# One of four edge-weight multiplications of a step goes from VectorE to GpSimd, in three groups of four

## The chip, the cores and the metric

The kernel runs on one core of a Trainium2 chip. The metric is the device time of one execution, in microseconds. Five engines work side by side, each in the order of its own queue: TensorE (PE in the profile, with its weight loads as PEld), VectorE (DVE), ScalarE (ACT), GpSimd (POOL) and the DMA issuing queue of SyncE (SP).

## The reference

Four graph layers follow each other on `x` of 128 graphs x 64 nodes x 256 features, each as `x = x + layer(relu(layernorm(x)))`. Only the fourth matters here, an attention over 512 edges (`src`, `dst`) with four heads of 64 features:

```python
Xq = (H @ W_lin.T).reshape(bt, n, h, dh)
Xv = (H @ W_val.T).reshape(bt, n, h, dh)
e = jnp.einsum('behd,hd->beh', jax.nn.leaky_relu(Xq[:, src] + Xq[:, dst], 0.2), a)
e = e + jnp.log(A0[src, dst] + EPS)[None, :, None]
e_t = e.transpose(1, 0, 2)
m = jax.ops.segment_max(e_t, src, num_segments=n)
ex = jnp.exp(e_t - m[src])
attn = ex / jax.ops.segment_sum(ex, src, num_segments=n)[src]
Vt = Xv[:, dst].transpose(1, 0, 2, 3)
Y = jax.ops.segment_sum(attn[..., None] * Vt, src, num_segments=n)
return Y.transpose(1, 0, 2, 3).reshape(bt, n, d) @ W_out.T
```

## The kernel before

`layer3` computes the fourth layer in 32 steps of 4 graphs, in `NG` = 4 groups of 8 steps. The edges are sorted, and gathering or summing over them is done by matmuls with one-hot matrices: `S2` (both ends of an edge, `ed_S` in the profile), `OST` and `ODT` (source and destination, edges on the partitions, four chunks `c` of 128 edges).

In an iteration `g` of the loop the following is issued, for different steps at once:

- `score`: 16 matmuls `ps<-ed_S,Q` into 8 PSUM tiles, read by ScalarE into `r`; `reduce` sums `r` into `acc` (`acc<-r,ed_apad`).
- `normed`, `turned`, `queries` for later blocks of 8 graphs: layer norm, transposes (`ps<-ident,h`, copied to `hT`, then differences `hS` and `hT<-hT` on VectorE), and the seven products for `Q` and `XV`, added up on VectorE.
- At the end of a group `summed`, `softmax` and `edgewise`: scans over `sm_m` and `sm_e` on VectorE, then the weights `at` of the next eight steps, with edges on the partitions.
- Ten iterations later, for step `v = g - 10`: `spread` multiplies the edge weights `at` with the one-hot `OST` on VectorE, both broadcast, to four tiles `aw` of 128 x 1024 (chunk pair `c` in 0, 2, graph pair half `x` in 0, 1); `gathered` contracts them with `ODT` in 32 matmuls (`ps<-aw,ed_ODT`), which ScalarE copies to `an`; `weighted` (`ps<-an,XV`) and `output` (`ps<-w_o,y`) follow a step later, and VectorE adds the product to `X`, which a DMA on SyncE's queue writes out.

In `gathered` the tiles are read in this order: for `c`, for the chunk `k` of the pair, for `x`. The pool of `aw` has five buffers, so a step's four tiles take the fifth and the first three of those before them, and a tile is written when the gather that reads its buffer's former contents is over. All PSUM tiles `ps` share seven buffers in turn.

In most iterations the order of VectorE's instructions follows a scheduler's priorities, with a few held places (`hold`). TensorE, VectorE and ScalarE are wrapped in `Ordered`, by whose helper nearly all instructions carry the line L799; GpSimd is not wrapped. The last ten steps are written out in `turn`, where the issue order of the three wrapped engines is that of the program (`nc.ordered = True`); it begins with step 22 (`v = 8 * NG - 10`), so that the last two steps of the third group fall into it.

Of the kernel before, what the change touches and what calls it, by code (L numbers as in the profile page):

```python
# [11 lines left out]
ALU = mybir.AluOpType  # L12
# [1430 lines left out]
B, N, D = 128, 64, 256  # L1443
P = 128
# [5 lines left out]
NG = 4  # L1450
# [15 lines left out]
class Kernel:  # L1466
# [1253 lines left out]
    def spread(self, st, g, c, pool, vp, sp, rp, psum, psc):  # L2720

        at, i = st["at", g // 8], g % 8
        W = []
        for x in range(2):
            w = vp.tile([P, 2, 8, N], F32, name="aw", bufs=5)
            self.o.mul(w[:], at[:, c:c + 2, x, i].rearrange("p c m h -> p c (m h)")[:, :, :, None]
                       .to_broadcast([P, 2, 8, N]), self.OST[:, c:c + 2, None, :].to_broadcast([P, 2, 8, N]))
            W.append(w)
        return W

# [106 lines left out]
```

## Time and profile before

| | us |
|---|---|
| median of 3 runs | 2264.54 (2262.23 to 2266.95) |
| profiled execution, time | 2267.39 |
| profiled execution, span from first to last instruction | 2265.6 |
| TensorE busy | 2222.2 (98%) |
| VectorE busy | 1611.1 (71%) |
| ScalarE busy | 1143.9 (50%) |
| GpSimd busy | 7.3 (33 instructions, all but one in the first 43 us) |
| all 128 `aw` multiplications on VectorE | 150.3 (1.219 each) |
| mean granted TensorE clock | 0.996 |

Times in the profile's lines are microseconds from the span's start, unless marked ns. A line of a timeline gives start, time, engine, line of the kernel, operation, what is written and read (names of tiles, with the numbers of buffers left out), shape and count; in square brackets is the idle time of the engine before it and what ended that. A line of a waits or groups view gives the same for many instructions together. A line of the windows view gives, for a stretch, its length and the busy time of PE, PEld, DVE, ACT and POOL with the number of instructions, then the granted clock, the DMA engines' share and GB/s. Matmuls are pipelined, and a matmul that waits for a buffer can show as a longer block of matmuls instead of as idle time.

### The profile page before, as it was taken

The page shows a single profiled execution, that of the slowest core. Times are in us where ns is not written, and L with a number is a line of the kernel's source. Part 1 is how long each engine was busy: PE and PEld are TensorE (multiplying, and loading weights), DVE is VectorE, ACT ScalarE, POOL GpSimd, SP SyncE. Part 2 cuts the span into 40 slices and gives each one's busy share as a digit, 9 for nine tenths or more (in the row PEclk, how much of TensorE's full clock was granted, in tenths as well). Part 3 has the DMA queues.
Part 4 walks back from the last instruction along what each step waited for, and adds up shares of the span by engine and source line. Part 5 has one row for each costly group of instructions (what it writes and reads, how often), then busy time and mean ns, then how long its engine had stood idle before and what let it go on. Part 6 is the DMA issues. An engine that isn't in the chain of part 4 may idle for free.

```text
span 2265.6 us, 33653 instructions
## 1 busy us (share of the span) xinstructions
PE 2222.2 (98%) x12617; PEld 1619.5 (71%) x12617; DVE 1611.1 (71%) x4068; ACT 1143.9 (50%) x2499; POOL 7.3 (0%) x33
## 2 busy tenths in 40 slices
PE   7999998999999999999999999999999999999999
PEld 4554444667777778888999999888887555555554
DVE  8877576888438786676766766666965688778667
ACT  5667864764436663444444444334533664444431
POOL 1000000000000000000000000000000000000000
PEclk9999999999999999999999999999999999999999
DMA  6000210121000000000100002000002000000001
GB/s 180 1 1 13 73 56 23 66 94 38 1 28 1 1 19 1 1 1 1 38 1 1 1 1 75 1 1 5 13 1 75 1 1 15 15 20 20 15 25 48
DMA packets 61070, 54.88 MB, mean 24 GB/s; under 512 B 15203, under 2 KB 58724, under 8 KB 60900
## 3 DMA queue, kind: packets, MB, share of 16 engines
q1 hardware_dynamic: 60900, 52.66, 7.5%
q8 instruction: 101, 1.65, 0.3%
q14 instruction: 69, 0.57, 0.1%
HBM read 35.86 MB, written 16.78 MB: 23 GB/s over the span
## 4 chain that ended last, share of the span: by engine, by line
PE 78%; DVE 4%; ACT 1%; issue 1%; ACTq 0%; DVEq 0%
PE ps L799 71%; PE pt L799 4%; PE acc L799 3%; DVE sm_m L799 1%; PE pe L799 1%; DVE aw L799 1%; DVE X L799 1%; DVE XV L799 0%; ACT ls_g L799 0%; ACT h L799 0%; DVE ls_g L799 0%; DVE lin_p L799 0%; DVE lin_s L799 0%; DVE hT L799 0%; DVE sm_e L799 0%
## 5 line engine op out<-in xcount | busy, mean ns | idle before, releaser
L799 ACT ACTIVATE ls_g<-ls_g,ls_b 128x512 f32<-128x512 f32 (+4 forms) x472 | 243.2, 565 | 154.7 <-DVE ls_g L799 152.9
L799 ACT ACTIVATE ls_g<-ps,ls_b 128x256 f32<-128x256 f32 (+3 forms) x268 | 115.3, 470 | 335.6 <-PE ps L799 332.5
L799 PE MATMUL ps<-z,w 128*128 128x512 f32 x512 | 257.2, 624 | 0.0
L799 PE MATMUL ps<-big,X 128*128 128x176 f32 (+3 forms) x848 | 212.7, 366 | 0.1
L799 DVE TENSOR_TENSOR ls_g<-ls_z,ps 128x512 f32<-128x512 f32 (+5 forms) x256 | 146.9, 579 | 91.6 <-PE ps L799 90.0
L799 PE MATMUL ps<-ls_tx,X 128*128 128x160 f32 (+2 forms) x960 | 206.8, 326 | 1.5 <-DVE ls_tx L799 0.9
L799 PE MATMUL ps<-X,X 128*128 128x160 f32 (+1 forms) x896 | 199.0, 306 | 0.0
L799 PE MATMUL ps<-X,ls_w 128*128 128x256 f32 x640 | 190.4, 379 | 0.0
L799 PEld LDWEIGHTS ps<-ls_tx,X 128*128 128x128 f32 x960 | 161.7, 190 | 16.4 <-DVE X L799 4.8
L799 DVE TENSOR_TENSOR aw<-at,ed_OST 128x1024 f32<-128x1024 f32 x128 | 150.3, 1219 | 28.7 <-PE ps L799 28.5
L799 PEld LDWEIGHTS ps<-big,X 128*128 128x128 f32 x848 | 146.0, 190 | 29.7 <-issue 19.4
L799 ACT ACTIVATE r<-ps 128x512 f32<-128x512 f32 x256 | 129.3, 625 | 63.0 <-PE ps L799 63.0
L799 DVE TENSOR_TENSOR X<-ls_g 128x1024 f32<-128x1024 f32 (+2 forms) x108 | 117.4, 1087 | 49.8 <-ACT ls_g L799 49.8
L799 PEld LDWEIGHTS ps<-X,X 128*128 128x128 f32 x896 | 148.5, 190 | 0.0
L799 PE MATMUL ps<-X,ls_s 128*128 128x256 f32 x480 | 142.3, 379 | 0.0
L799 PEld LDWEIGHTS ps<-z,w 128*128 128x128 f32 x512 | 87.6, 191 | 67.8 <-issue 60.6
L799 PE MATMUL ps<-ls_tx,ls_s 128*128 128x256 f32 x464 | 134.7, 379 | 0.0
L799 PEld LDWEIGHTS ps<-X,ls_w 128*128 128x128 f32 x640 | 121.4, 190 | 16.8 <-DVE X L799 0.3
L799 PE MATMUL ps<-ls_tx,ls_w 128*128 128x256 f32 x464 | 133.3, 380 | 0.1
L799 PE MATMUL ps<-big,ls_w 128*128 128x256 f32 x464 | 131.9, 379 | 0.8 <-ACT ls_z L799 0.8
L799 PE MATMUL ps<-ed_S,Q 64*128 64x512 f32 x512 | 121.4, 604 | 2.2 <-DVE hT L799 1.3
L799 PE MATMUL ps<-aw,ed_ODT 128*32 128x512 f32 x1024 | 121.7, 593 | 0.1
(552 smaller groups left out, 3946.4 us busy)
## 6 DMA issues: line engine op xcount, KB each, us to landing
X<-in_x_dram SPq DMA_DIRECT2D x32, 512.0 KB
xs<-X SPq DMA_DIRECT2D x16, 512.0 KB
X<-xs SPq DMA_DIRECT2D x16, 512.0 KB
out_dram<-X SPq DMA_DIRECT2D x31, 256.0 KB
X<-in_L_gnn_Wih_t_dram SPq DMA_DIRECT2D x4, 512.0 KB
ls_w<-in_L_gnn_Wih_t_dram SPq DMA_DIRECT2D x4, 512.0 KB
ls_w<-in_L_gnn_Whh_t_dram SPq DMA_DIRECT2D x4, 512.0 KB
w<-in_L_gnn_W_t_dram SPq DMA_DIRECT2D x2, 512.0 KB
```

The source lines that it names most:

```text
L799: i = method(*a, **kw)
```

## The change

In `spread`, the tile with `c + x == 3` (that is `c` = 2 and `x` = 1, the last of the four) is multiplied by GpSimd instead of VectorE when the step is below `8 * NG - 8` = 24, that is in the first three groups. These are 24 of the 128 multiplications. The operands, the result and the buffers are the same. As GpSimd isn't wrapped, its instructions are in no written order with those of the other engines, and wait by semaphores alone.

```diff
         W = []
         for x in range(2):
             w = vp.tile([P, 2, 8, N], F32, name="aw", bufs=5)
-            self.o.mul(w[:], at[:, c:c + 2, x, i].rearrange("p c m h -> p c (m h)")[:, :, :, None]
-                       .to_broadcast([P, 2, 8, N]), self.OST[:, c:c + 2, None, :].to_broadcast([P, 2, 8, N]))
+            engine = self.nc.gpsimd if c + x == 3 and g < 8 * NG - 8 else self.nc.vector
+            engine.tensor_tensor(w[:], at[:, c:c + 2, x, i].rearrange("p c m h -> p c (m h)")[:, :, :, None]
+                                 .to_broadcast([P, 2, 8, N]), self.OST[:, c:c + 2, None, :].to_broadcast([P, 2, 8, N]),
+                                 op=ALU.mult)
             W.append(w)
         return W
```

## The prediction

> **What bounds the kernel now.** I read the page first, for shares; then the busy time of the stretch in which the weighted one-hots are made; then the timelines of TensorE (PE) and VectorE (DVE) there; and last GpSimd's few early instructions, the only rows that say what this engine costs.
>
> The page (busy time, and the group of the multiplication that is moved):
>
> ```profile
> PE 2222.2 (98%) x12617; PEld 1619.5 (71%) x12617; DVE 1611.1 (71%) x4068; ACT 1143.9 (50%) x2499; POOL 7.3 (0%) x33
> L799 DVE TENSOR_TENSOR aw<-at,ed_OST 128x1024 f32<-128x1024 f32 x128 | 150.3, 1219 | 28.7 <-PE ps L799 28.5
> ```
>
> One `aw` is 1.22 us on DVE, 1.13 us from one start to the next when several follow each other. Busy time of steps 0 to 23, in the order PE, PEld, DVE, ACT, POOL:
>
> ```profile
> 1862.00:2210.00 348.00, 347.00 (x2810) 199.25 (x2808) 265.58 (x438) 157.62 (x311) 0.00 (x0) 1.00 0.05 18
> ```
>
> PE is busy 347.0 of 348.0 us at granted clock 1.00, DVE 265.6. So less DVE work is worth only what PE loses to DVE. A late buffer mostly shows as a longer PE block, so I compare blocks of one kind (PE timeline):
>
> ```profile
> 1904.55 3.70 PE L799 MATMUL ps<-ed_S,Q 64*128 64x512 f32 x16
> ...
> 1966.03 3.81 PE L799 MATMUL ps<-ed_S,Q 64*128 64x512 f32 x12
> 1970.31 1.13 PE L799 MATMUL ps<-ed_S,Q 64*128 64x512 f32 x4 [0.47 <-DVE X L799]
> ...
> 2207.66 4.78 PE L799 MATMUL ps<-aw,ed_ODT 128*32 128x512 f32 x32
> ```
>
> Sixteen score matmuls take 3.63 us from start to next start; at 1966 they take 5.34 (1.70 lost), and the same block at 2089.70 takes 5.17 (1.53 lost). Both are group boundaries: DVE runs without a pause from 1940.17 to 1970.59 (softmax, norm, `aw`), and its `hT` copy and `X` addition free PSUM banks late. The gather at 2207.66 takes 4.71 against 3.75 (0.96 lost, to `aw`). Some 0.2 us more stands near 2198 to 2203. That is all: 1.70 + 1.53 + 0.96 + 0.2 = 4.4 us, 0.19% of the time. Nothing that relieves DVE here can give more.
>
> An odd step on DVE, away from a boundary:
>
> ```profile
> 1899.97 3.50 DVE L799 TENSOR_TENSOR aw<-at,ed_OST 128x1024 f32<-128x1024 f32 x3 [3.13 <-PE ps L799]
> 1903.39 0.68 DVE L799 COPY hT<-ps 128x512 f32<-128x512 f32 x1
> 1903.99 1.22 DVE L799 TENSOR_TENSOR aw<-at,ed_OST 128x1024 f32<-128x1024 f32 x1
> 1905.12 0.42 DVE L799 TENSOR_TENSOR hS<-hT 128x256 f32<-128x256 f32 x1
> 1905.46 0.68 DVE L799 TENSOR_TENSOR X<-X,ps 128x512 f32<-128x512 f32 x1
> 1906.06 0.42 DVE L799 TENSOR_TENSOR hT<-hT 128x256 f32<-128x256 f32 x1
> ```
>
> The first `aw` waits 3.13 us for the running gather (1898.04 to 1901.79) to free a buffer; then four `aw` run, with `hT` between. `X` ends at 1906.14. At 1970 the score block ended 1.12 us after `X` did, so here `X` may end up to 1904.55 + 3.63 - 1.12 = 1907.06 before PE is late: 0.9 us of slack.
>
> GpSimd, at the start of the kernel, beside DVE instructions with two operands in SBUF:
>
> ```profile
> 37.64 0.21 DVE L799 SCALAR_TENSOR_TENSOR f_h_t<-f_h_r,f_x,f_h_s 64x1 f32<-64x1 f32 x1
> 38.45 0.20 POOL L1811 TENSOR_TENSOR ed_key<-ed_key,ed_less 128x4 f32<-128x4 f32 x1
> 40.13 1.49 POOL L1807 TENSOR_SCALAR big<-big 128x512 f32<-128x512 f32 x1
> 41.70 1.27 POOL L1808 TENSOR_TENSOR big<-big 128x512 f32<-128x512 f32 x1
> 41.91 1.07 DVE L799 SCALAR_TENSOR_TENSOR f_h_t<-f_h_r,f_x,f_h_s 64x1 f32<-64x1 f32 x1
> ```
>
> The same one-element DVE instruction takes 0.21 us alone and 1.07 us when GpSimd's TENSOR_TENSOR has begun: it ends at 42.98, GpSimd at 42.97. So it stood until about 42.98 - 0.21 = 42.77. DVE work with one operand in SBUF (statistics at 41.59, 0.40 us) was not held up.
>
> **The change part by part.** *GpSimd's price.* 1.27 us for 512 columns, 0.20 for 4: 2 x 1.27 - 0.20 = 2.34 us for 1024. DVE is shut out 42.77 - 41.70 = 1.07 us of the 512-column one, so about 2.14 us. The lower bound is DVE's own 1.22, the upper one twice the 1.49 of TENSOR_SCALAR, 2.98. I take 2.34 and 2.14, because that row is the same operation with the same kind of operands; broadcast operands are in no GpSimd row.
>
> *When it runs.* Fourth tile of step v takes the buffer of the third tile of step v-1 (4 tiles a step, 5 buffers), which gather v-1 frees about 3.5 us after its start. Ready at worst 3.5 + 0.7 + 2.3 = 6.5 us after that start. Gathers stand 11 us apart at least (1869.41, 1880.40), and the tile is read by the last third of the next one, 2.4 us in. So PE does not wait for GpSimd: some 6.9 us of cover; without it each microsecond late would be paid 24 times. GpSimd's queue holds nothing else here, no DMA moves, and PE's order is unchanged.
>
> *Removed from DVE.* 24 x 1.13 = 27 us, of which at most the 4.4 us above can come back.
>
> *Added to DVE.* When GpSimd becomes ready (gather start + 3.5), DVE is always in its second `aw` (from +3.1 to +4.2), with the third, the next step's first, right behind; that one reads two SBUF operands. Whoever gets the port first makes the other wait. No row shows this contest. I take GpSimd first, as its request is then 0.7 us old while DVE's third `aw` has still to be issued; the other order is a rival. Then DVE's third `aw` is 2.14 us later, and all behind the removed `aw` is 2.14 - 1.13 = 1.0 us later. By kind of step:
> - Even steps: XV, now 1.0 us later, has 1.5 us in hand (second XV addition ended at 1888.69, its bank was needed at 1890.22). Nothing.
> - Odd steps away from boundaries, 8: `X` is 1.0 us later, and in the changed instruction order it comes behind `hT<-hT` (0.35 us more). 1.35 - 0.9 = 0.45 us each: 3.6 us.
> - First odd step (1872.84): there is no output product yet, so the `hT` copy itself gates the score block (ended 1876.92, weights loaded at 1876.97, no slack). It stands in front of the removed `aw`, so it moves by the full 2.14: 2.1 us.
> - Two boundaries: the multiplication of the step before holds up the third `aw` and so the scans and XV by 2.14 us; XV's slack (1.0 us there: 1950.49 against 1951.52) is used up, so PE loses 1.1 us. One `aw` less at 1952.54 and one less at 1964.64 give back 2.26. The next GpSimd multiplication falls at about 1964 and shuts out `sm_e` and `aw` for 1.2 us. With `X` behind `hT`, and one instruction's wait more, `X` ends 1.45 us later than now: 2 x 1.45 = 2.9.
> - End of the third group: at 2198.1 GpSimd (step 23) delays the second `aw` by 2.1, the sums behind it by 1.0 and PE by 1.0; the 0.96 us at 2207.66 disappears, as `at` comes no later than now. 0.1.
>
> Sum: 3.6 + 2.1 + 2.9 + 0.1 = +8.7 us. The profiled execution is 2267.39 us (span 2265.6 and 1.8 around it), 2.85 over the median of 2264.54; 2276.1 by it, 2273.2 by the median.
>
> The Trainium skill bears on this: "SBUF — State Buffer", section "Who interferes with whom", says that a DVE instruction with two SBUF inputs and a GpSimd instruction that reads SBUF exclude each other, and that the first holds the port for its whole instruction. The trace agrees on the exclusion but releases DVE 0.2 us before GpSimd's end (42.77 against 42.97). By the rule the shut-out would be the full 2.34 us, and 12 places times 0.2 would make the sum about 11 us. I keep the row's 2.14.
>
> **The rivals.**
> 1. *DVE's third `aw` goes first.* It is back to back with the second (1.13 us apart), which may leave GpSimd no opening. Then GpSimd runs under `hT` and the scans, which read PSUM. `hS` waits 0.4 us, odd steps stay inside their 0.9 us, each boundary is 0.25 us worse, the end gains 1.1: 0.5 - 1.1 = -0.6 us, 2263.9.
> 2. *Faster: the port hardly matters.* For it: DVE's 0.66 us at 40.15 beside TENSOR_SCALAR was a short delay, though GpSimd ran on until 41.62. Then `X` at the boundaries is 1.9 us earlier (two `aw` less, 2.26, minus 0.35), more than the 1.70 and 1.53 lost, and the end gains 0.96 + 0.2: -4.4 us, 2260.1. It decides if DVE loses well under 0.95 us to each GpSimd multiplication: two such losses eat the boundary's 1.9. Against it: the 1.07 us row.
> 3. *GpSimd at its upper bound*, 2.98 us, shutting DVE out for 2.8: 0.65 us more at 8 odd steps, the first one and two boundaries (7.2), and even steps pass their 1.5 us by 0.2 (1.6): 8.7 + 8.8 = 17.5 us, 2282.
>
> That the change does nothing is excluded: 24 multiplications stand in GpSimd's instruction order and 24 are missing from DVE's.
>
> **How the numbers follow.** Forecast 0.43 (its own range 2269 to 2277: stalls of 0 to 0.8 us at the 8 odd steps), rival 1 0.25, rival 2 0.20, rival 3 0.12. A measurement can tell about 0.2%, 4.5 us, from no change. Slower: 0.43 + 0.12 = 0.55. Rival 2 lies at the bound itself; I count 0.12 of it beyond and 0.08 within, so the same is 0.25 + 0.08 = 0.33. The range takes in the ceiling of the gain and rival 3: 2260 to 2282.
>
> **What would show it.** GpSimd: 24 `aw` of 2.2 to 2.5 us (longer where they wait for the port). Right: one DVE `aw` per step of about 3.3 us, score blocks of some 4.1 us in odd steps, 1.4 us more than now at the boundaries. Rival 1: all DVE `aw` near 1.2 us and longer `hS`. Rival 2: nothing longer, score blocks of 3.63 us at both boundaries. The prediction is wrong if DVE's rows keep their lengths, or if gathers wait for GpSimd.

## The result, and the profile after

The changed kernel takes 2269.62 us (median of 9 runs, 2267.51 to 2274.47) against 2264.54 (9 runs, 2261.45 to 2267.33): +5.1 us, ratio 1.0025, 95% interval 1.0016 to 1.0033. The direction was right; the forecast was +8.7 us. The profiled execution is 2272.24 us with a span of 2270.5.

The page of the changed kernel, busy time and the multiplications left on VectorE:

```profile
PE 2221.6 (98%) x12617; PEld 1609.2 (71%) x12617; DVE 1621.1 (71%) x4044; ACT 1144.9 (50%) x2499; POOL 63.3 (3%) x57
L799 DVE TENSOR_TENSOR aw<-at,ed_OST 128x1024 f32<-128x1024 f32 x104 | 158.8, 1573 | 29.8 <-PE ps L799 29.5
```

VectorE has 24 `aw` fewer and is busy 10 us longer: the 104 left take 1.57 us on average instead of 1.22. The windows view of the same stretch shows what PE makes of it:

```profile
1862.00:2210.00 348.00, 341.17 (x2732) 186.09 (x2734) 270.96 (x404) 156.44 (x307) 55.93 (x24) 1.00 0.05 17
```

PE's busy time falls from 347.0 to 341.2 us at the same granted clock; TensorE now has gaps in which it waits. The odd step that the prediction showed, on VectorE and on GpSimd (timelines):

```profile
1900.93 5.20 DVE L799 TENSOR_TENSOR aw<-at,ed_OST 128x1024 f32<-128x1024 f32 x3 [3.13 <-PE ps L799]
1906.06 0.68 DVE L799 COPY hT<-ps 128x512 f32<-128x512 f32 x1
1906.77 0.42 DVE L799 TENSOR_TENSOR hS<-hT 128x256 f32<-128x256 f32 x1
1907.30 0.42 DVE L799 TENSOR_TENSOR hT<-hT 128x256 f32<-128x256 f32 x1
1907.64 0.68 DVE L799 TENSOR_TENSOR X<-X,ps 128x512 f32<-128x512 f32 x1
```

```profile
1861.99 2.74 POOL L2727 TENSOR_TENSOR aw<-at,ed_OST 128x1024 f32<-128x1024 f32 x1 [1495.85 <-ACT Q L799]
1902.69 2.36 POOL L2727 TENSOR_TENSOR aw<-at,ed_OST 128x1024 f32<-128x1024 f32 x1 [15.15 <-PE ps L799]
...
1945.87 2.31 POOL L2727 TENSOR_TENSOR aw<-at,ed_OST 128x1024 f32<-128x1024 f32 x1 [10.49 <-PE ps L799]
...
2203.94 1.90 POOL L2727 TENSOR_TENSOR aw<-at,ed_OST 128x1024 f32<-128x1024 f32 x1 [4.22 <-PE ps L799]
```

Three `aw` that took 3.50 us take 5.20: the third is 1.70 us longer (2.92 instead of 1.22). GpSimd starts at 1902.69, waits about 0.4 us for the second `aw`, runs, and only then does the third one run. When GpSimd does not have to wait it takes 1.90 us (2203.94). TensorE's timeline at a group start, in that odd step, at the first boundary and at the end:

```profile
1863.01 4.58 PE L799 MATMUL ps<-ed_S,Q 64*128 64x512 f32 x16
...
1905.50 4.01 PE L799 MATMUL ps<-ed_S,Q 64*128 64x512 f32 x16
...
1953.33 1.13 PE L799 MATMUL ps<-w_t,hT 128*128 128x256 f32 x4 [0.50 <-DVE XV L799]
...
1956.01 3.70 PE L799 MATMUL ps<-ed_S,Q 64*128 64x512 f32 x16 [0.62 <-ACT Q L799]
...
1968.54 1.99 PE L799 MATMUL ps<-ed_S,Q 64*128 64x512 f32 x8
1970.79 1.13 PE L799 MATMUL ps<-ed_S,Q 64*128 64x512 f32 x4 [0.27 <-DVE hT L799]
1972.84 1.13 PE L799 MATMUL ps<-ed_S,Q 64*128 64x512 f32 x4 [0.92 <-DVE X L799]
...
2213.50 3.77 PE L799 MATMUL ps<-aw,ed_ODT 128*32 128x512 f32 x32
```

The odd step's score block (1905.50 to 1909.44) takes 3.94 us instead of 3.63. At the boundary the score block still loses what it lost before (1968.54 to 1973.90, 5.36 against 5.34), and two new waits of 0.50 and 0.62 us, for XV and what follows from it, stand ahead of it. The last gather has lost its wait: 3.70 from start to next start instead of 4.71.

To place all of it I compare the starts of each step's gather in the two traces, and take the change from one gather to the next. (The time up to the layer's first score, where the code is the same, varied by over 6 us from one profiled execution to another, so it is left out.) From the first score on, the changed kernel's profiled execution is 5.45 us longer than that of before:

| part | forecast | measured |
|---|---|---|
| group starts, steps 0, 8, 16 | 0 | +0.88, +0.61, +0.61 = +2.10 |
| first odd step | +2.1 | +0.80, then -0.13 = +0.67 |
| odd steps away from boundaries | 8 x 0.45 = +3.6 | 7 x 0.30 (one of them, step 13, from TensorE's order), less 0.20 after five = +1.1 |
| two boundaries | +2.9 | 1.18 + 1.46 = +2.64 |
| end of the third group | +0.1 | +0.19 - 0.30 - 1.01 = -1.12 |
| sum | +8.7 | +5.4 |

### The profile page after: what moved, and what is told of

It reads as the page before. It is cut to its first block, busy times and chain, and to the rows that moved or that the text cites. A ratio compares the mean times of both kernels' runs of the same rounds, so it can differ in the third digit from the quotient of the medians.

```text
span 2270.5 us, 33700 instructions
## 1 busy us (share of the span) xinstructions
PE 2221.6 (98%) x12617; PEld 1609.2 (71%) x12617; DVE 1621.1 (71%) x4044; ACT 1144.9 (50%) x2499; POOL 63.3 (3%) x57
## 4 chain that ended last, share of the span: by engine, by line
PE 75%; DVE 6%; issue 1%; ACT 1%; DMA 0%; DVEq 0%; ACTq 0%
PE ps L799 68%; PE pt L799 4%; PE acc L799 3%; DVE aw L799 1%; DVE sm_m L799 1%; PE pe L799 1%; DVE X L799 1%; DVE XV L799 1%; ACT ls_g L799 0%; DVE hT L799 0%; ACT h L799 0%; DVE n_st L799 0%; DVE lin_p L799 0%; DVE lin_s L799 0%; DVE hS L799 0%
## 5 line engine op out<-in xcount | busy, mean ns | idle before, releaser
L799 DVE TENSOR_TENSOR aw<-at,ed_OST 128x1024 f32<-128x1024 f32 x104 | 158.8, 1573 | 29.8 <-PE ps L799 29.5
```

Of the source, the lines that this page charges most:

```text
L799: i = method(*a, **kw)
```

## The experiments

Each was timed beside the kernel before. "Layer" is the change from the first score to the end, in the one profiled execution. As the time ahead of the layer varies by more than most of these effects, the layer and the gathers tell more than the medians: in runs 6 and 7 the steps away from the change agree with the kernel before to 0.02 us.

**1. GpSimd only writes.** Is it the port, or the changed instruction order?

```diff
+            if c + x == 3 and g < 8 * NG - 8:
+                self.nc.gpsimd.memset(w[:], 0.0)
+                W.append(w)
+                continue
```

> The 24 tiles keep their buffers, waits and places, but GpSimd only writes zeros into them: the product of that quarter is left out, and GpSimd reads nothing from SBUF. Port theory (GpSimd's reading shuts out VectorE instructions with two SBUF operands): all aw on VectorE stay at 1.22 us, score blocks of odd steps 3.63 us, the 1.70 and 1.53 us lost at the two boundaries and the 0.96 us at the end go away; 4.4 us below the kernel before, 2260. Order theory (the changed order, X behind hT, and the waits between two engines cost the time): nothing changes against the changed kernel, score blocks of 3.93 us in odd steps, some 5 us above the kernel before, 2269.5.

Measured: 2261.83 us (11 runs) against 2264.45, ratio 0.9986 (0.9977 to 0.9995); layer -3.73. Groups and GpSimd's timeline of this run:

```profile
L799 DVE TENSOR_TENSOR aw<-at,ed_OST 128x1024 f32<-128x1024 f32 x104 | 122.1, 1220 | 30.0 <-PE ps L799 29.8
```

```profile
1899.37 0.95 POOL L2727 MEMSET aw<- 128x1024 f32 x1 [16.74 <-PE ps L799]
```

With the same 24 instructions gone from VectorE and the same tiles written by GpSimd, no `aw` is longer than 1.23 us and the steady steps change by 0.00, but for +0.28 at step 13. So the changed order costs those 0.28 us and no more, and it is the reading that costs. The gain is what the prediction had as its ceiling: -1.61 and -1.29 at the boundaries, -1.13 at the end (4.4 had been counted).

**2. A step ahead.** Two tags of buffers (`aw` 3, `awg` 2); GpSimd makes its tile of the next step after copying one element of `hS` (odd steps) or `lin` (even steps) into it, when VectorE has no two-input work; the first step of each group is VectorE's.

```diff
+            self.ahead(st, v + 1, st["sums", g // 2 + 1][2][:, 0:1], pools[1])
...
+        w = st["aw", g] = vp.tile([P, 2, 8, N], F32, name="awg", bufs=2)
+        self.nc.gpsimd.tensor_copy(w[:, 0, 0, 0:1], after)
+        self.nc.gpsimd.tensor_tensor(w[:], ...
```

> GpSimd makes its tile one step ahead and starts when VectorE comes to a pause: after the last hS of a step for odd steps, after the copies to lin for even ones (a one-element GpSimd copy of that result into the tile is put before the multiplication). VectorE makes the first step of each group itself; buffers are split 3 + 2. Port theory: VectorE's aw are all about 1.22 us, as GpSimd's 1.9 us fall into VectorE's pauses and under instructions with one SBUF operand; the boundaries lose their 1.70 and 1.53 us and the end gains 1 us: 3 to 4.4 us below the kernel before, 2260 to 2261.5. Order theory: the same work on GpSimd costs as much wherever it stands, no gain over the kernel before, 2264.5 or above.

Measured: 2265.08 us, ratio 1.0003 (0.9994 to 1.0012); layer -0.64. By the time alone this is the order theory's result; the gathers say otherwise. GpSimd takes 1.90 us a tile, and steady steps change by 0.00: where nobody asks for the port, the same 1.90 us of GpSimd are free. The boundaries gave only -0.85 and -0.53: the tile for the step after the scans came too late by 0.4 us, and with three buffers VectorE's `aw` were pushed into the boundary. At the end +0.75 was lost, where step 23's tile was not held back and one `aw` ahead of the scans took 2.92.

**3 and 4. Which steps cost.** The 24 tiles split in two halves of 12: `g % 8` in 0, 1, 6, 7, and in 2 to 5.

```diff
-            engine = self.nc.gpsimd if c + x == 3 and g < 8 * NG - 8 else self.nc.vector
+            engine = self.nc.gpsimd if c + x == 3 and g < 8 * NG - 8 and not 2 <= g % 8 <= 5 else self.nc.vector
```

> GpSimd multiplies only in steps 0, 1, 6 and 7 of each of the three groups, 12 of the 24 tiles. By the differences between the two traces, gather by gather, the cost stands there: 0.88 + 0.80 + 1.11 + 0.07 in the first group, 0.61 + 0.30 + 1.32 + 0.14 in the second, 0.61 + 0.32 in the third, -1.1 at the end: 5.1 us above the kernel before, 2269.6. If each multiplication costs alike (5.1 / 24 = 0.21 us): 2.5 us above, 2267.

> GpSimd multiplies only in steps 2 to 5 of each of the three groups, the other 12 tiles. By the differences gather by gather: a score block that is 0.30 us longer and an acc block behind it that is 0.20 us shorter, 0.1 us for two steps, 0.4 us in all: 2265, the same as before. If each multiplication costs alike: 2.5 us above, 2267.

Measured: the edges 2268.50 us, ratio 1.0015 (1.0006 to 1.0024), layer +3.45; the steady steps 2267.27, ratio 1.0007 (0.9998 to 1.0016), layer +0.65. The times alone do not decide: 2267.27 is what the steady steps were to take if each multiplication cost alike, and 2268.50 lies between the two figures for the edges. The gathers do: in the steady steps each odd step is 0.30 longer and the next one 0.20 shorter. So the edges carry most of the loss; the two layers' sum, 4.1, is 1.35 short of the changed kernel's 5.45. Most of that is one place: in the edges' run the first boundary cost nothing (-0.23 where the changed kernel has +1.18). There, as in two steps of the other run, VectorE's third `aw` went first; timelines of GpSimd at that boundary of the edges' run, and of GpSimd and VectorE in such a step of the steady run:

```profile
1942.29 3.72 POOL L2727 TENSOR_TENSOR aw<-at,ed_OST 128x1024 f32<-128x1024 f32 x1 [70.28 <-PE ps L799]
```

```profile
1885.55 3.63 POOL L2727 TENSOR_TENSOR aw<-at,ed_OST 128x1024 f32<-128x1024 f32 x1 [1517.95 <-PE ps L799]
```

```profile
1883.94 3.48 DVE L799 TENSOR_TENSOR aw<-at,ed_OST 128x1024 f32<-128x1024 f32 x3
```

VectorE's three take 3.48 us as before, GpSimd waits 1.73 us of its 3.63, and VectorE loses nothing. (That such a step costs PE nothing says little in the steady run, as both are even steps, which lose nothing in the changed kernel either; the boundary says it.) This is rival 1 of the prediction, seen in three places, and in none of the changed kernel's 24.

**5. Under the scans.** As experiment 2, with four buffers for VectorE and one for GpSimd; the tile for step 6 of a group is released by that step's third VectorE tile, so that it runs beside the scans.

```diff
+            w = vp.tile([P, 2, 8, N], F32, name="awg" if c + x == 3 else "aw", bufs=1 if c + x == 3 else 4)
...
+            if c + x == 3 and g < 21 and i == 6:
+                engine.tensor_copy(w[:, 0, 0, 0:1], W[0][:, 0, 0, 0:1])
```

> The same 24 tiles on GpSimd but other places for them: each is made a step earlier, released by a one-element copy that GpSimd makes from hS (odd steps) or from the Q and XV products (even steps), when VectorE has no two-input work left; the tile of step 6 of each group is released by the same step's third VectorE tile, so that it runs under the scans; steps 21 to 23 are not held back. Buffers are four for VectorE's tiles and one for GpSimd's; the first step of each group stays on VectorE (so 21 tiles on GpSimd). Port theory (the loss is VectorE's third aw waiting 1.70 us for the shared port): steady steps 0, group boundaries -1.6 and -1.5, end about -1, in all -4 us: ratio 0.998, about 2260.5. Rival (GpSimd costs something wherever it runs, and the first form of this shift gave only what VectorE had lost anyway): ratio 1.000 or above, 2264.5 or more.

Measured: 2260.78 us (11 runs) against 2264.14, ratio 0.9983 (0.9974 to 0.9992); layer -3.61. It is faster than both kernels. Timelines of GpSimd, VectorE and TensorE at the first boundary:

```profile
1946.24 1.90 POOL L2736 TENSOR_TENSOR awg<-at,ed_OST 128x1024 f32<-128x1024 f32 x1
```

```profile
1942.64 3.48 DVE L799 TENSOR_TENSOR aw<-at,ed_OST 128x1024 f32<-128x1024 f32 x3
1946.03 1.21 DVE L799 TENSOR_TENSOR_SCAN sm_m<-ed_drop,acc 128x512 f32<-128x512 f32 x1
1947.16 1.19 DVE L799 TENSOR_TENSOR_SCAN sm_m<-ed_dropr,acc 128x512 f32<-128x512 f32 x1
```

```profile
1965.49 4.04 PE L799 MATMUL ps<-ed_S,Q 64*128 64x512 f32 x16
```

The multiplication lies wholly beside two scans, which keep their 1.2 us (their second operand, `acc`, is in PSUM), and the boundary's score block falls from 5.34 us to 3.97.

**6 and 7. The group starts and the end by themselves.** GpSimd has the fourth tile of steps 0, 8 and 16 only, or of 22 and 23 only.

```diff
+            engine = self.nc.gpsimd if c + x == 3 and g in (0, 8, 16) else self.nc.vector
```

```diff
+            engine = self.nc.gpsimd if c + x == 3 and g in (22, 23) else self.nc.vector
```

> Only the first step of each of the three groups (steps 0, 8, 16) has its fourth tile on GpSimd: 3 of the 24. Theory A (what I had left out of my sum: there GpSimd starts with VectorE's first tiles, and the XV addition or the first gather is late by it): +0.9, +0.6, +0.6 = +2.1 us in the profile's gaps between gathers, ratio 1.001. Rival B (that +2.1 comes from the steps that follow, 1, 9 and 17): below +0.5 us, ratio 1.000.

> Only steps 22 and 23, the last two of the third group, have their fourth tile on GpSimd: 2 of the 24. Theory A (one aw less on VectorE before the scans gives back the wait of the gather at 2207, and the shut-out comes where VectorE is not late): -1.1 us in the profile's gaps at the end, ratio 0.9995. Rival B (the gain at the end in the changed kernel came from earlier steps being late): 0, ratio 1.000.

Measured: group starts 2266.98 us, ratio 1.0005 (0.9996 to 1.0014); end 2263.83, ratio 1.000 (0.9991 to 1.001). Both times are inside what the measurement can't tell apart; the gathers do tell. The three group starts cost +0.88, +0.61 and +0.61 as in the changed kernel, of which 0.42, 0.20 and 0.20 come back in the next step: layer +1.31. The end gives +0.16 - 0.30 - 0.99 = -1.13, as in the changed kernel. So both terms stand by themselves.

**8. Twice.** GpSimd multiplies each of its tiles two times.

```diff
+            for _ in range(2 if engine is self.nc.gpsimd else 1):
```

> GpSimd multiplies each of its 24 tiles twice, with the same result, so its cost is doubled and nothing else changes. Theory A (the loss of a steady step is small only because slack swallows most of 1.70 us; a second 1.70 finds none): odd steps +1.5 us more each (7 of them, 10 us), even steps over their slack by some 0.7 (10 of them, 7 us), first steps of the groups and the boundaries 1.7 more each (10 us): in all 20 to 30 us above the changed kernel, 2290 to 2300. Rival B (VectorE does not wait for the second multiplication, since it gets the port between the two, or its slack covers it): below +8 us over the changed kernel, under 2278.

Measured: 2297.78 us (4 runs), ratio 1.0147 (1.0132 to 1.0163): 28 us above the changed kernel, inside the 20 to 30 expected, but not made up as expected. Even steps lost nothing and odd steps away from boundaries +1.28 instead of +0.30; most of the loss stands at the first odd steps (+3.3, +4.4, +5.9) and at the boundaries' score blocks (+4.6, +4.6). Timelines of VectorE and TensorE in an odd step:

```profile
1901.73 5.20 DVE L799 TENSOR_TENSOR aw<-at,ed_OST 128x1024 f32<-128x1024 f32 x3 [3.13 <-PE ps L799]
1906.86 0.68 DVE L799 COPY hT<-ps 128x512 f32<-128x512 f32 x1
1907.57 1.41 DVE L799 TENSOR_TENSOR hS<-hT 128x256 f32<-128x256 f32 x1
```

```profile
1910.15 1.13 PE L799 MATMUL ps<-ed_S,Q 64*128 64x512 f32 x4 [1.01 <-DVE X L799]
```

The three `aw` take 5.20 us, no longer than with one multiplication: VectorE got the port between the two, and the second ran under `hT`, so that only `hS`, which reads two SBUF operands, waited 1.0 us. That is a part of rival B's mechanism; its price was wrong.

**9 and 10. A later request.** GpSimd first clears the tile (0.95 us, which does not disturb VectorE) and then multiplies; in 10 the first step of each group is left to VectorE.

```diff
+            if engine is self.nc.gpsimd:
+                engine.memset(w[:], 0.0)
```

> The same 24 tiles on GpSimd, but ahead of each multiplication GpSimd clears the tile with a memset (0.95 us, write only), so that its request for the port comes about 1 us later, inside VectorE's third aw instead of its second. Nothing else is changed, and GpSimd has more work than in the changed kernel. Theory A (what costs is that GpSimd goes ahead of the third aw): that aw is 1.22 us again, GpSimd runs under the hT copy and the scans, odd steps lose nothing, boundaries gain 1.6 and 1.5, the end about 1; the group starts still lose (+0.9, +0.6, +0.6, with 0.2 to 0.4 given back each): about -2.5 us against the kernel before, 2261.5 to 2262.5. Rival B (GpSimd's 1.90 us are lost wherever they fall, so later is no better): +4 us or more, 2268 and above.

> As the run with the memset ahead, but the first step of each group (0, 8, 16) stays on VectorE: 21 tiles on GpSimd. Theory A: the group starts' loss is gone too, about -4 us against the kernel before, ratio 0.998. Rival B: +3 us or more.

Measured: 2266.84 us, ratio 1.0009 (1.0000 to 1.0019), layer +2.0; and 2265.17, ratio 0.9997 (0.9989 to 1.0006), layer +1.2. Timelines of GpSimd and VectorE in run 9, the odd step and the first boundary:

```profile
1899.31 2.48 POOL L2729 TENSOR_TENSOR aw<-at,ed_OST 128x1024 f32<-128x1024 f32 x1
...
1960.61 2.55 POOL L2729 TENSOR_TENSOR aw<-at,ed_OST 128x1024 f32<-128x1024 f32 x1
```

```profile
1896.53 3.50 DVE L799 TENSOR_TENSOR aw<-at,ed_OST 128x1024 f32<-128x1024 f32 x3 [3.13 <-PE ps L799]
...
1960.19 4.05 DVE L799 TENSOR_TENSOR aw<-at,ed_OST 128x1024 f32<-128x1024 f32 x2
```

Away from the edges theory A held to the hundredth: three `aw` take 3.50 us, and the steps that cost +0.30 and -0.20 now cost 0.00, though GpSimd does 50% more. In these odd steps the multiplication runs under `hT`, and `hS` behind it waits 1.0 us (1.41 instead of 0.42), which the slack takes. Both sums missed: the layer was to fall by some 2.5 and 4 us. I had taken the boundaries' gain of 1.6 and 1.5 whole, but the multiplication after the scans still meets an `aw` there (1960.61: two take 4.05 us; in run 5 it was 2.35), and these boundaries gave +0.08 and +0.41. The first odd step lost 0.80 in run 9, and 1.70 in run 10, since there step 0's fourth `aw` on VectorE put GpSimd's request into the second of the three.

## Why the prediction was right, step by step

**The mechanism** is the forecast one. GpSimd's request comes during VectorE's second `aw`, GpSimd goes first, and the third `aw` pays. Experiment 1 (same order, no reading: -2.6 us) and experiment 5 (the same reading, other places: -3.4) leave no other cause for the loss but 0.28 us at step 13 (below). As forecast, PE's waits name no GpSimd instruction. Rival 1's order is in none of the 24; rival 2 is out, as the port does matter, and rival 3 is out, as GpSimd takes 1.90 us and not 2.98.

**GpSimd's price** was too high: 2.34 us forecast, 1.90 measured; VectorE's loss 2.14 forecast, 1.70 measured. The 512-column row at the kernel's start (1.27 us, twice, less 0.20) does not scale to this shape. The two differ in more than size, as these operands are broadcast; which of that matters was not tried. That GpSimd's recorded 2.3 us look like the forecast 2.34 is luck: 0.4 of them are its wait for the second `aw`.

**Odd steps** were the largest wrong term: 3.6 forecast, 1.1 measured. I counted 8, and 7 lose time (3, 5, 9, 11, 13, 17, 19); the eighth, step 21, has no `hT` copy ahead of `X` and loses nothing. Each was put at 0.45 and is 0.30, where two errors nearly cancel: 0.44 less from GpSimd's price, but the removed `aw` ahead of X gave 0.47 (1.70 later by the third `aw`, X 1.23 later in its step) and not 1.13 - 0.35 = 0.78, as `hS` and `hT`, now one behind another, start with pauses. And I had not seen that 0.20 comes back in the following gather: it takes 3.55 us instead of 3.75 when the score block ahead of it was late, which the trace of before already has behind its own late block (3.55 at 1973.73); why is not shown. Step 13's +0.3 is not the port's: 0.28 of it stands in runs 1, 3 and 5 too, where no `aw` of that step is held up. The prediction took PE's order as unchanged, and here it is not: one `acc` matmul now stands behind the gather's first three. TensorE in the kernel before, then in the changed one:

```profile
2052.13 3.82 PE L799 MATMUL ps<-aw,ed_ODT 128*32 128x512 f32 x32
...
2058.62 3.70 PE L799 MATMUL ps<-ed_S,Q 64*128 64x512 f32 x16
```

```profile
2055.45 0.61 PE L799 MATMUL ps<-aw,ed_ODT 128*32 128x512 f32 x3
2055.52 0.59 PE L799 MATMUL acc<-r,ed_apad 128*32 128x512 f32 x1
2055.88 3.67 PE L799 MATMUL ps<-aw,ed_ODT 128*32 128x512 f32 x29
...
2062.23 3.73 PE L799 MATMUL ps<-ed_S,Q 64*128 64x512 f32 x16
```

The score block starts 6.78 us after the gather instead of 6.49, and takes 3.66 itself, so the late `X` costs hardly anything more. In run 4, where PE's order is the old one, the same step loses 0.31 to the port.

**The first odd step**, 2.1, came to 0.67. Its score block is 1.18 us longer: 1.70 less 0.53, by which the three `aw` start earlier, since step 0's fourth `aw` is gone from in front of them; I had held that it would move by the full amount. The gather ahead of it was 0.38 shorter.

**Group starts** were left out of the sum. There GpSimd's first multiplication starts with VectorE's (1861.99, 2.74 us), the second `aw` takes 2.32 and the XV addition behind it frees its bank 1.10 us later in the score block, which takes 4.51 us (VectorE's timeline):

```profile
1863.49 2.32 DVE L799 TENSOR_TENSOR aw<-at,ed_OST 128x1024 f32<-128x1024 f32 x1
1865.74 0.67 DVE L799 TENSOR_TENSOR XV<-XV,ps 128x512 f32<-128x512 f32 x1
```

Experiment 6 shows these +2.1 alone; I had looked at where the pattern is steady and not at where a group begins.

**Boundaries**: 2.9 forecast, 2.64 measured. XV was to cost PE 1.1 us, and the first boundary's step has +1.11, but that agreement is partly luck. XV's second addition ended 1.44 us later after the gather's start and not 2.14, and beside PE's wait of 0.50 for it stands one of 0.62 for `Q`, which the sum did not have; on the other side the gather ahead was 0.21 shorter, and the 0.21 that the step's score block had lost before (3.84 us) is gone. At the second boundary, where that block had lost nothing before, the step has +1.32. The score block behind the scans was to lose another 0.35 each, and the first one is unchanged (5.36 us against 5.34); from gather to gather the two give +0.07 and +0.14.

**The end**: +0.1 forecast, -1.12 measured. The 0.96 us of the last gather came back as forecast, but little of the loss before it came. Step 22's multiplication fell beside scans, which it does not hold up, and not beside an `aw` (2197.41). Step 23's (2203.94) did make the second `aw` 1.73 us longer, but the two started 0.45 earlier in the step, as one `aw` less stood ahead of the scans, and part of the rest went into a wait of 0.56 that VectorE had there before: what follows came 0.65 later, and the next gather 0.19 instead of 1.0.

In all, odd steps were priced 2.5 too high, the first odd step 1.4, boundaries 0.3 and the end 1.2, and 2.1 of group starts were left out: the sum was 3.3 too high. The terms that the sum had came to 3.3 and not to 8.7; that the total came nearer is due to the one left out.

## What to carry to other kernels

Work moved from VectorE to GpSimd is not free because GpSimd is idle: price it by what VectorE loses where both read two SBUF operands, 1.70 us for 1.13 us saved here, and then ask in each place what stands behind the instruction that waits. If the helper's instruction can be placed into VectorE's pauses or beside VectorE work that reads PSUM (here two beside scans, most others in pauses), nearly the same multiplications (21 of the 24) turn from +5.1 us to -3.4. Sum over every kind of place, group starts and ends among them, for the steady steps, which are most, made here only 1.1 us of the 5.4.

## What the runs showed of the hardware

- A GpSimd instruction that only writes does not hold VectorE up: 24 memsets of 0.95 us left two-operand `aw` at 1.22 us. The Trainium skill says this too ("SBUF — State Buffer", section "Who interferes with whom": a two-input VectorE instruction contends with a GpSimd instruction that reads SBUF, not with one that only writes it), and the run agrees.
- GpSimd's recorded time includes its wait for the port: 2.3 us in steady steps, 2.74 at group starts and up to 3.72, where 1.90 is its own.
- Which of the two goes first is not settled by who starts first. GpSimd, starting 0.62 to 0.67 us into a running `aw`, went ahead of the next one each time that one followed directly; three times in runs 3 and 4 it had started 0.39 to 0.48 us into one, and VectorE's next went ahead. But in runs 9 and 10, behind a memset, starts of 0.10 and 0.42 us went ahead too, and in run 8 one of 0.41 without a memset. The section just named says that the order of issue decides who blocks; those three do not fit it, unless the recorded start is not the request. What decides stays open.
